# A dilated 7x7 convolution with softmax and gather: sorting of x shared anew, weights copied before the products, factors applied in other places

## The chip, the cores and the metric

The kernel runs on one core of a Trainium2 chip, in float32 throughout. The metric is the device time of one execution in microseconds (us). In the profile PE is TensorE (matmuls), PEld its loads of the stationary operand, DVE is VectorE, ACT ScalarE, POOL GpSimd, and SP the engine that issues most transfers. A "q" behind an engine's name is its sequencer, which issues transfers and waits.

## The reference, cut to what matters

```python
# x: (4, 256, 64, 64)
k = conv(x, w1, padding=6, rhs_dilation=2) + b1         # 128 channels, 7x7 taps
k = conv(k, w2) + b2                                    # 1x1: 49 channels
attn = softmax(k, axis=1)
xp = pad(x, 6)
shifts = stack([xp[:, :, 2*u:2*u+64, 2*v:2*v+64] for u in range(7) for v in range(7)], 1)
x = einsum('bkchw,bkhw->bchw', shifts, attn)            # gather
# second layer, a bottleneck with batch statistics
h = relu(bn(conv1x1(x, m1), g1, be1))
h = relu(bn(conv3x3(h, m2), g2, be2))
h = bn(conv1x1(h, m3), g3, be3)
out = relu(h + x)
```

No bias or activation stands between w1 and w2, so the kernel multiplies w1 by w2 first and convolves once, from 256 channels to 49 logits.

## The kernel before, in words

**The dilated convolution in passes.** Along the image's rows the seven taps are not multiplied one by one. Four numbers p (PAIRS = 0.4, 0.8, 1.25, 2.5) are points of a Toom-Cook scheme: for each pass the rows of x are summed with polynomial coefficients into two images, "even" and "odd" rows' sums mixed as x0 + p x1 and x0 - p x1; matmuls with weights evaluated at +p and -p follow, and the results are put together to four output rows. A fifth pass takes the points zero and infinity. Passes are numbered 0 to 4.

**Buffers.** One SBUF tile, `arena`, holds three regions: `slots`, the rows of x of 128 channels, sorted by parity so that a polynomial is a sum of shifted rows; `xi`, the two summed images of the pass at hand; and `ut`, the weights at all points. Columns are cut into four strips (32 columns of each column parity, eight to a strip). `visit` (L232) makes `xi` for some strips with `transform`, a series of multiply-adds on VectorE, all in the helper `stt` on L151. `apply_factor` (L226) works on `slots` in place: each row becomes the next row of its parity minus p^2 times the row, for a p whose pass is done, so that later passes have shorter sums. It is applied by parities (0 and 1) and strips. `column_convs(s)` (L251, matmuls on L262) adds one strip's products into eight PSUM banks: 200 matmuls for the four strips.

**Two halves of the channels.** The five passes run over the first 128 channels, and each pass's sums are put aside in DRAM (`put_aside`, L281, a copy on L286 and a transfer on L287, both on ScalarE). Then the five passes run over the other 128 channels. For these each strip's sums are put back into PSUM (`put_back`: a transfer on SP, L606, and a copy on ScalarE, L607), matmuls add to them, and `outputs` (copy L590 on ScalarE, L591 to L600 on VectorE) adds them into the four rows' logits.

**The opening.** x is loaded in twelve transfers (three pieces of rows times four images, `piece`, L344) and w1 in two times two (`load_w1`, L316). `sort_x` (L160) writes a piece into `slots` with four copies, recorded on L170: two parities k times two sub-rows a. Three run on ScalarE, and k=1, a=1 on GpSimd. `early` (L350) makes parts of pass 0's sums for the output rows that the pieces at hand allow. `product` (L319) forms the merged weights for one of seven columns of taps v: seven matmuls (L325) whose stationary operand is a slice of `w1raw` with a step of 49 elements, two evacuations on ScalarE (L336, L337), and two additions on VectorE (L341, L342). Seven products belong to the first half of the channels; after strips 0 and 1 of pass 0 the seven products of the second half follow on TensorE.

**What sets the order.** Within these stages the order of the instructions is that of the code: a manual schedule covers VectorE and TensorE in the first half, ScalarE and SP too in the opening (L365 on), and all four at the turns (L676 on). Each engine takes its own queue in order. GpSimd's order is the scheduler's. Small loads are issued on ScalarE's queue; those of `bn12` and `bn3` (L501 to L503) belong to tiles of the pool `keep`, made at the very start.

**Staging.** During passes 1 to 4 of the first half VectorE also prepares the second half: `fill_stage` sorts the other 128 channels into `stage`, `stage_parts` (L442) makes pass 0's sums for them, strip by strip into one buffer `stage_x`, and stores each as 1 MB in `ready_dram`; `stage_rows` (L450) stores the sorted rows in `fsort_dram`. The second half reads both.

**Turns.** After the softmax (`exponents` with the exponential on L527, `shares` with L534 to L540), `turn` (L555) transposes one half-strip's shares on TensorE (L566) and copies them into `amat`: for each of four j, part g=0 and part g=1, both on ScalarE (L573), except that with `shared` part g=1 is copied on VectorE (L571). The gather (L752) follows.

## Time and profile before

| | us |
|---|---|
| three runs | 800.84, 800.90, 802.21 |
| median | 800.9 |
| the profiled execution's own time | 799.53 |
| its span | 797.6 |
| TensorE busy | 729.1 |
| VectorE busy | 574.6 |
| ScalarE busy | 297.7 |
| GpSimd busy | 75.7 |

The span runs from the first to the last recorded instruction of the execution, and the execution's own time is 1.93 us longer. Times in the trace count from the start of the span. In round numbers the stages of the trace are: the opening to 55 us, pass 0 of the first half and the second half's products to 121.6, passes 1 to 4 to about 272, the second half to about 472, softmax and turns to about 499, gather and first 1x1 convolution to 657, and the rest of the bottleneck to 797.6. "A <- B" after a wait says that A stood idle until B had ended; a group's row in the profile's fifth part has its busy time, the mean of one instruction in ns, and the idle time before it.

### The profile page before, as it was taken

The numbers are of one execution on the slowest core, as the hardware profiler recorded it, in microseconds if no ns is written. First come the engines' busy times: TensorE is split into PE (matmuls) and PEld (weight loads), VectorE is DVE, ScalarE is ACT, GpSimd is POOL, SyncE is SP. The second block draws the span as 40 slices with busy tenths as digits, with TensorE's granted clock in tenths as the row PEclk, the third lists the DMA queues.
The fourth block names the chain that finished last, engine by engine and source line by source line (L and its number), as shares of the span: only waits on it lengthen the run. The fifth ranks groups of instructions, "written<-read, shape, count | busy, mean of one in ns | idle before, by whom it ended". The sixth has DMA issues, their size and how long they took to land.

```text
span 797.6 us, 10675 instructions
## 1 busy us (share of the span) xinstructions
PE 729.1 (91%) x4080; PEld 590.2 (74%) x4080; DVE 574.6 (72%) x682; ACT 297.7 (37%) x594; POOL 75.7 (9%) x143
## 2 busy tenths in 40 slices
PE   0949999999999999988999999999999979979996
PEld 0938977888888888867888888988887854438742
DVE  4489989999666999999999867233341337663697
ACT  4640155112551101110111158434442446345497
POOL 3210010001000020000002113222222200000000
PEclk9979999999999999998999999999999998998997
DMA  7941089913898886210210013666766669361298
GB/s 290 373 162 41 0 292 297 382 57 126 287 341 349 311 307 233 71 41 11 60 37 16 2 57 101 202 220 212 229 234 212 212 238 342 108 196 39 85 391 367
DMA packets 59236, 150.24 MB, mean 188 GB/s; under 512 B 7346, under 2 KB 35634, under 8 KB 55090
## 3 DMA queue, kind: packets, MB, share of 16 engines
q1 hardware_dynamic: 51216, 141.11, 49.7%
q10 hardware_dynamic: 7970, 8.45, 3.0%
q8 instruction: 32, 0.52, 0.3%
q14 instruction: 18, 0.15, 0.1%
HBM read 93.81 MB, written 55.74 MB: 188 GB/s over the span
## 4 chain that ended last, share of the span: by engine, by line
PE 72%; DVE 15%; ACT 5%; DMA 4%; issue 2%; POOL 0%; SPq 0%; ACTq 0%; DVEq 0%; POOLq 0%
PE acc L262 42%; PE acc L752 13%; DVE arena L151 9%; PE acc L785 4%; PE pconv L964 3%; PE pdirect L952 3%; DVE arena L1070 3%; PE acc L566 2%; PE moments L1030 2%; PE acc L325 2%; ACT outer L1075 1%; DMA outer<-in_xt_dram 1%; ACT arena L573 1%; DMA w1raw<-in_w_dram 1%; PE pturn L1026 1%
## 5 line engine op out<-in xcount | busy, mean ns | idle before, releaser
L262 PE MATMUL acc<-arena 128*128 128x343 f32 (+3 forms) x2000 | 380.2, 353 | 20.5 <-DVE arena L151 20.5
L262 PEld LDWEIGHTS acc<-arena 128*128 128x128 f32 x2000 | 321.6, 192 | 78.1 <-issue 15.7
L151 DVE SCALAR_TENSOR_TENSOR arena<-arena 128x1024 f32<-128x1024 f32 (+7 forms) x192 | 290.5, 1554 | 24.7 <-PE acc L262 14.2
L752 PEld LDWEIGHTS acc<-arena,outer 128*128 128x128 f32 x1024 | 116.0, 193 | 11.3 <-issue 10.1
L752 PE MATMUL acc<-arena,outer 128*128 128x128 f32 x1024 | 118.8, 277 | 3.1 <-issue 2.9
L793 DVE BATCH_NORM_STATS2 st<-acc 128x6 f32<-128x512 f32 x16 | 11.2, 699 | 68.2 <-PE acc L785 68.0
L286 ACT COPY sv<-acc 128x392 f32<-128x392 f32 x40 | 19.1, 484 | 99.2 <-PE acc L262 87.3
L170 ACT COPY stage<-raw 128x128 f32<-128x128 f32 x128 | 43.6, 415 | 23.9 <-DMA raw<-in_xp_dram 23.5
L325 PE MATMUL acc<-powers,w1raw 128*128 128x196 f32 (+1 forms) x196 | 45.3, 394 | 6.6 <-DMA w1raw<-in_w_dram 5.0
L325 PEld LDWEIGHTS acc<-powers,w1raw 128*128 128x128 f32 x196 | 44.5, 314 | 7.1 <-issue 7.0
L590 ACT COPY outer<-acc 128x784 f32<-128x784 f32 x8 | 6.5, 812 | 101.8 <-PE acc L262 101.8
L1013 PE MATMUL pconv<-arena,w3m 64*128 64x512 f32 (+1 forms) x144 | 43.0, 587 | 0.6 <-DVE arena L1070 0.6
L123 ACT COPY outer<-outer 64x2048 f32<-64x2048 f32 x15 | 28.4, 1895 | 38.4 <-DMA outer<-in_xt_dram 38.4
L151 DVE SCALAR_TENSOR_TENSOR outer<-outer 128x784 f32<-128x784 f32 (+2 forms) x47 | 36.8, 835 | 3.6 <-ACT outer L906 3.6
L1013 PEld LDWEIGHTS pconv<-arena,w3m 64*128 64x128 f32 x144 | 20.7, 185 | 21.9 <-DVE arena L1070 16.0
L1075 ACT ACTIVATE outer<-arena 128x512 f32<-128x512 f32 (+1 forms) x58 | 34.7, 695 | 1.3 <-DVE arena L849 1.1
L773 DVE COPY bks<-acc 128x256 f32<-128x256 f32 x32 | 11.3, 417 | 32.5 <-PE acc L752 32.5
L1070 DVE SCALAR_TENSOR_TENSOR arena<-pconv,arena 128x512 f32<-128x512 f32 (+1 forms) x58 | 34.3, 667 | 0.0
L124 POOL COPY outer<-outer 64x1792 f32<-64x1792 f32 x15 | 25.1, 1676 | 95.5 <-DMA outer<-in_xt_dram 80.1
L607 ACT COPY acc<-bks 128x392 f32<-128x392 f32 x40 | 18.5, 488 | 40.7 <-DVE outer L592 33.8
L573 ACT COPY arena<-acc 128x512 f32<-128x512 f32 x52 | 27.1, 708 | 14.8 <-PE acc L566 14.4
L964 PE MATMUL pconv<-outer,arena 128*128 128x512 f32 x72 | 31.1, 592 | 0.0
(143 smaller groups left out, 627.7 us busy)
## 6 DMA issues: line engine op xcount, KB each, us to landing
raw<-in_xp_dram SPq DMA_DIRECT2D x36, 608.0 KB, 5.3
outer<-in_xt_dram SPq DMA_DIRECT2D x17, 896.0 KB, 6.3
out_dram<-outer SPq DMA_DIRECT2D x14, 1024.0 KB, 4.5
arena<-y_dram SPq DMA_DIRECT2D x25, 512.0 KB, 7.9
fsort_dram<-stage SPq DMA_DIRECT2D x2, 4864.0 KB, 14.7
arena<-fsort_dram SPq DMA_DIRECT2D x8, 1216.0 KB, 10.0
y_dram<-outer SPq DMA_DIRECT2D x16, 512.0 KB, 5.4
aside_dram<-sv ACTq DMA_DIRECT2D x40, 196.0 KB, 5.7
```

What stands on the lines that cost most here:

```text
L123: nc.scalar.copy(t[:MID], x[MID:])
L151: nc.vector.scalar_tensor_tensor(out, in0, scalar, in1, ALU.mult, ALU.add)
L170: (last if last and k + a == 2 else nc.scalar.copy)(d[:, k, :, PLACE[b], 2 * a : 2 * a + 2, i : i + count], raw[:, lo : lo + 4 * count - 3 ...
L262: nc.tensor.matmul(acc[i][d][:, o : o + (hi - lo) * K], xi[:, i, CW * w : CW * w + CW, :].rearrange("p x t -> p (x t)"), u[i][:, lo * K : ...
L325: nc.tensor.matmul(pw[:, o : o + n], w1raw[:, :, u * K7 + v], powers[:, u, :n], start=(u == 0), stop=(u == K7 - 1), skip_group_check=True,)
L573: nc.scalar.copy(dst, src)
L752: nc.tensor.matmul(dst[:, :: NT - 1] if edge else pts[c][:, o : o + 128], x[:, i, half * P : (half + 1) * P], amat[:, b % 2, :, c, blocks, ...
L785: nc.tensor.matmul(pt[a * MID : (a + 1) * MID, :], w1m[:, n, :], ys[a, n][:, 512 * i : 512 * i + 512], start=(n == 0), stop=(n == NH - 1), ...
L964: nc.tensor.matmul(m[k], wu[:, k, j, :], vs[k][:, g, j : j + R, :], start=(j == 0), stop=(j == 1))
L1013: nc.tensor.matmul(pt[:, :n], w3m[part, half * P : (half + 1) * P], h2[part, slot, q, lo : lo + n], start=True, stop=True)
L1070: nc.vector.scalar_tensor_tensor(v, conv3(b, q, i, half, lo, n), sc3[:, half : half + 1], v, ALU.mult, ALU.add)
L1075: nc.scalar.activation(dst, v.rearrange("p (r w) -> p r w", w=R), AF.Relu, bias=sh3[:, half : half + 1])
```

## The change

- `bn12` and `bn3` become tiles of the pool `late`. Their ten loads are now issued after that of `w3m`, still on ScalarE's queue.
- `piece` is split into `load_piece` and `sort_piece`. In piece 1 of each image the copy k=0, a=0 runs on VectorE, in piece 2 on GpSimd, so that ScalarE has two of the four copies. Piece 2 is sorted by halves of the columns: strips 0 and 1 first, strips 2 and 3 after `early(1, strip(2, 2))`. The products of the first half and the calls of `early` are ordered anew among them.
- In a product of the second half, ScalarE first copies the seven taps (7 x 128 elements) out of `w1raw` into a buffer `w1v` of the pool of raw pieces, and the stationary operands are read from there, without a step.
- The factor of pass 1 is applied to strips 0 and 1, parity 0, ahead of pass 0's sums of strips 2 and 3; to parity 1 after the third product of the second half; and to strips 2 and 3 in pass 1, ahead of their `visit`.
- `stage_parts` stores each parity as soon as it is made, in two transfers of 0.5 MB.
- In turns (1, 1) and (2, 0) part g=1 of odd j is copied on VectorE: four copies.
- In the second half the factor of pass 2 is applied to strips 0 to 2 within pass 1, each after the next strip's `visit`; strip 3 keeps its place.

```diff
--- before.py
+++ after.py
@@ -101,8 +101,6 @@
 
 
     keep = pool(ctx, "keep", 1)
-    bn12 = keep.tile([P, 4], F32, name="bn12")
-    bn3 = keep.tile([P, 2, NH], F32, name="bn3")
     st1 = keep.tile([P, 2 * NT, 6], F32, name="st1")
 
 
@@ -157,7 +155,7 @@
 
     zero_rows(slots)
 
-    def sort_x(raw, b, r0, n, dst, w0, last=None):
+    def sort_x(raw, b, r0, n, dst, w0, last=None, first=None):
 
         d = dst.rearrange("p k (w b e) i -> p k w b e i", b=B, e=Q)
         nw = d.shape[2]
@@ -167,7 +165,7 @@
             i = (m + 3) // 2
             for a in range(2):
                 lo = 2 * m + a - r0
-                (last if last and k + a == 2 else nc.scalar.copy)(
+                (last if last and k + a == 2 else first if first and k + a == 0 else nc.scalar.copy)(
                     d[:, k, :, PLACE[b], 2 * a : 2 * a + 2, i : i + count],
                     raw[:, lo : lo + 4 * count - 3 : 4, PAD + 2 * w0 : PAD + 2 * w0 + 2 * nw].rearrange(
                         "p r (w c) -> p w c r", c=2
@@ -318,13 +316,19 @@
 
             def product(w1raw, half, v, pw):
 
+                wv = w1raw[:, :, v::K7].rearrange("p c u -> p u c")
+                if half:
+                    t = rawp.tile([P, 24, WP], F32, tag="raw", name="w1v").rearrange("p r w -> p (r w)")
+                    t = t[:, : K7 * P].rearrange("p (u c) -> p u c", c=P)
+                    nc.scalar.copy(t, wv)
+                    wv = t
                 for u in range(K7):
 
                     o = 0 if u == 0 else (2 + NP) * K if u % 2 else K
                     n = (1 + NP) * K if u in (0, K7 - 1) else NP * K
                     nc.tensor.matmul(
                         pw[:, o : o + n],
-                        w1raw[:, :, u * K7 + v],
+                        wv[:, u, :],
                         powers[:, u, :n],
                         start=(u == 0),
                         stop=(u == K7 - 1),
@@ -341,11 +345,16 @@
                 nc.vector.tensor_tensor(ut[:, half, 1 + NP : 1 + 2 * NP, c], ue, uo, ALU.subtract)
                 nc.vector.tensor_tensor(ue, ue, uo, ALU.add)
 
-            def piece(n, b):
+            def load_piece(n, b):
                 r0, k = PIECES[n]
                 raw = rawp.tile([P, 24, WP], F32, tag="raw", name="raw")
                 nc.sync.dma_start(out=raw[:, :k], in_=xp[b, :P, r0 : r0 + k, :])
-                sort_x(raw, b, r0, k, slots, 0, nc.gpsimd.tensor_copy)
+                return raw
+
+            def sort_piece(raw, n, b, cols=0, strips=NS):
+                r0, k = PIECES[n]
+                first = (None, nc.vector.tensor_copy, nc.gpsimd.tensor_copy)[n]
+                sort_x(raw, b, r0, k, slots[:, :, strip(cols, strips)], WS * cols, nc.gpsimd.tensor_copy, first)
 
             def early(n, cols=slice(None), parts=(even, odd, mix)):
 
@@ -364,47 +373,48 @@
             spare = [acc[i][s] for s in (NS - 1, 0) for i in range(2)]
             with tc.manual_schedule(engines={mybir.EngineType.Activation, mybir.EngineType.SP}):
                 for b in range(B):
-                    piece(0, b)
+                    sort_piece(load_piece(0, b), 0, b)
                 w1a = load_w1(0)
                 early(0)
                 nc.scalar.copy(b1row, b1sb.to_broadcast([P, P]))
                 nc.tensor.matmul(bank[7][:, :K], b1row, w2sb, start=True, stop=False)
                 nc.tensor.matmul(bank[7][:, :K], ones, b2sb, start=False, stop=True)
                 nc.scalar.copy(bias, bank[7][:, :K])
-                for b in range(2):
-                    piece(1, b)
-                    product(w1a, 0, b, bank[b])
-                for b in range(2, B):
-                    piece(1, b)
-                early(1, strip(0, 2), (even,))
-                for v in range(2, 5):
-                    if v > 2:
-                        piece(2, v - 3)
+                for b in range(B):
+                    if b == 3:
+                        product(w1a, 0, 0, bank[0])
+                    sort_piece(load_piece(1, b), 1, b)
+                for v, part in ((1, even), (2, odd)):
+                    early(1, strip(0, 2), (part,))
                     product(w1a, 0, v, bank[v])
-                early(1, strip(0, 2), (odd, mix))
-                piece(2, 2)
+                raws = []
+                for b in range(B):
+                    raws.append(load_piece(2, b))
+                    sort_piece(raws[b], 2, b, 0, 2)
+                early(1, strip(0, 2), (mix,))
+                product(w1a, 0, 3, bank[3])
+                product(w1a, 0, 4, bank[4])
+                early(2, strip(0), (even, odd))
                 product(w1a, 0, 5, bank[5])
-                piece(2, 3)
-                early(2, strip(0), (even, odd))
+                early(2, strip(0), (mix,))
                 product(w1a, 0, 6, bank[6])
-                early(2, strip(0), (mix,))
                 w1b = load_w1(1)
             early(2, strip(1))
             early(1, strip(2, 2))
+            for b in range(B):
+                sort_piece(raws[b], 2, b, 2, 2)
+            apply_factor(slots, squares[0], NR - 1, strip(0, 2), (0,))
             for s in range(2, NS):
                 early(2, strip(s))
             u = weights(0, 0)
             column_convs(0, u, True)
             column_convs(1, u, True)
             put_aside(0, 1)
-            product(w1b, 1, 0, spare[0])
-            apply_factor(slots, squares[0], NR - 1, strip(0, 2))
-            for v in range(1, 5):
+            for v in range(3):
                 product(w1b, 1, v, spare[v % 4])
-            apply_factor(slots, squares[0], NR - 1, strip(2, 2), (0,))
-            for v in range(5, K7):
+            apply_factor(slots, squares[0], NR - 1, strip(0, 2), (1,))
+            for v in range(3, K7):
                 product(w1b, 1, v, spare[v % 4])
-            apply_factor(slots, squares[0], NR - 1, strip(2, 2), (1,))
         for s in range(2, NS):
             column_convs(s, u, True)
             put_aside(0, s)
@@ -443,9 +453,9 @@
             for s in strips:
                 x = stgp.tile([P, 2, SW, NT], F32, tag="x", name="stage_x")
                 row = rows_of(stage, strip(s))
-                even(PAIRS[0], squares, row, x[:, 0])
-                odd(PAIRS[0], squares, row, x[:, 1])
-                nc.sync.dma_start(out=ready[:, 2 * h + s], in_=x)
+                for i, part in enumerate((even, odd)):
+                    part(PAIRS[0], squares, row, x[:, i])
+                    nc.sync.dma_start(out=ready[:, 2 * h + s, i], in_=x[:, i])
 
         def stage_rows(h):
             nc.sync.dma_start(out=fsort[:, h], in_=stage)
@@ -457,8 +467,8 @@
                 continue
             u = weights(n, 0)
             for h in range(2):
-                if factor is not None and factor != squares[0]:
-                    apply_factor(slots, factor, NR - 2, strip(2 * h, 2))
+                if factor is not None and (n, h) != (1, 0):
+                    apply_factor(slots, factor, NR - 1 if n == 1 else NR - 2, strip(2 * h, 2))
                 visit(slots, strip(2 * h, 2), p, left)
                 if (n, h) == (2, 1):
                     stage_parts(0, [0])
@@ -490,6 +500,8 @@
     w3m = late.tile([P, C], F32, name="w3m")
     pavg_sb = late.tile([P, P], F32, name="pavg_sb")
     pdiff_sb = late.tile([P, P], F32, name="pdiff_sb")
+    bn12 = late.tile([P, 4], F32, name="bn12")
+    bn3 = late.tile([P, 2, NH], F32, name="bn3")
     nc.scalar.dma_start(out=ident, in_=z)
     nc.scalar.dma_start(out=w1m, in_=m1t)
     nc.scalar.dma_start(out=pavg_sb, in_=pavg)
@@ -567,7 +579,7 @@
             for g in range(2):
                 dst = amat[:, g, 2 * (2 * s + h) + j % 2, j // 2].rearrange("p (n k) e -> p k n e", k=2)
                 src = pt[:, :, 64 * g : 64 * g + 64].rearrange("p (k w) n -> p k n w", k=2)
-                if shared and g:
+                if g and (shared or (j % 2 and (s, h) in ((1, 1), (2, 0)))):
                     nc.vector.tensor_copy(dst, src)
                 else:
                     nc.scalar.copy(dst, src)
@@ -630,10 +642,12 @@
             for t in pads:
                 nc.gpsimd.memset(t, 0.0)
         for s in range(NS):
-            if n == 2:
+            if n == 2 and s == NS - 1:
                 apply_factor(slots, factor, NR - 2, strip(s))
             if p is not None:
                 visit(slots, strip(s), p, left)
+            if n == 1 and s:
+                apply_factor(slots, passes[2][1], NR - 2, strip(s - 1))
             for d in ([s] if s == 0 else []) + ([s + 1] if s + 1 < NS else []):
                 put_back(n, d)
             column_convs(s, u, False)
```

## The prediction

> **What bounds the kernel now.** I read the page's busy shares first, then the waits, the chain of waits, and the busy time by windows of the stages that the change touches.
>
> ```profile
> PE 729.1 (91%) x4080; PEld 590.2 (74%) x4080; DVE 574.6 (72%) x682; ACT 297.7 (37%) x594; POOL 75.7 (9%) x143
> ```
>
> TensorE is busy for 91% of the span, so 68 us are all that a better order can win, and no edit here takes matmuls away. The waits (us in total, times, longest) say where VectorE holds TensorE up in the dilated conv:
>
> ```profile
> PE acc L262 <- DVE arena L151: 20.5, 3, 11.5
> ...
> DVE stage_x L151 <- DMA ready_dram<-stage_x: 6.2, 1, 6.2
> ```
>
> The trace puts the three at 43.4–54.9 (11.5), 118.6–121.6 (3.0) and 355.3–361.3 (6.0). The chain of waits (start, length) shows the two long stretches in which nothing but matmuls counts:
>
> ```profile
> 1.17 5.96 DMA b1sb<-in_b_dram
> 7.15 4.09 DMA raw<-in_xp_dram
> 11.26 9.69 DMA w1raw<-in_w_dram
> ...
> 121.63 224.88 PE acc L262 x1200
> ...
> 361.26 97.75 PE acc L262 x512
> ```
>
> What is won ahead of 121.63 reaches 346 only if VectorE keeps pace until then. The windows (PE, PEld, DVE, ACT, POOL busy, clock, DMA share, GB/s) tell how much room it has:
>
> ```profile
> 33.28:54.90 21.62, 10.90 (x50) 10.61 (x49) 16.81 (x25) 12.42 (x23) 4.65 (x4) 0.86 0.63 248
> 121.63:200.00 78.37, 78.37 (x415) 66.48 (x416) 77.75 (x36) 21.86 (x60) 2.56 (x4) 1.00 0.58 213
> 253.50:346.60 93.10, 93.10 (x496) 79.08 (x496) 89.87 (x68) 14.86 (x29) 3.99 (x1) 1.00 0.60 215
> ```
>
> In the opening VectorE idles 4.8 of 21.6 us; later it is as full as TensorE.
>
> **What the Trainium skill says.** "TensorE: Matmul & The Clock Gate", "LDWEIGHTS (loading the stationary operand)", has the load's time scale with the column count only. The trace disagrees for a strided source: 314 ns out of w1raw (elements 196 bytes apart, L325), 192 ns out of contiguous memory (L262); the measurement decides. "SBUF — State Buffer", "Door 1: The DMA port swizzle", says that an engine pays for each new 16-byte line. That agrees: the raw copies take 870 ns for 384 elements and spacings of 0.57 us for 256, some 1.75 ns per further element; the contiguous copy of L123 takes 1895 ns for 2048 (0.9). The same page, "Who interferes with whom", has VectorE with two SBUF inputs and GpSimd lock each other out; the trace agrees: GpSimd's 384-element copy takes 867 ns alone and 1420–1622 beside VectorE's additions, which then take 1477 and 1573 instead of about 1050.
>
> **The change part by part.** All times are the profiled execution's.
>
> ```profile
> L170 ACT COPY arena<-raw 128x384 f32<-128x384 f32 x24 | 19.1, 870 | 12.2 <-DVE arena L151 12.2
> ...
> L151 DVE SCALAR_TENSOR_TENSOR arena<-arena 128x4608 f32<-128x4608 f32 x4 | 19.7, 4951 | 0.0
> ```
>
> 1. *Tiny loads.* ACT's queue no longer begins with ten small loads, and in the built order raw loads 3 and 4 and the first w1 transfer wait for nothing; before, load 3 went out at 7.15, when b1 had landed. Up to the end of w1a 5.70 MB move at 396 GB/s (window 13–33): 14.4 us and some 4 for issue and first landing, 18.4 instead of 20.95, **−2.4**. The pieces of x follow on SP's queue, whose order of loads doesn't change.
> 2. *Sorting.* ACT copies 2 of 4 parts of a piece instead of 3, 1.6 us instead of 2.4; VectorE takes one of a piece 1 (estimate 0.45 each, from its 0.41 for 245–256 elements), GpSimd a second of a piece 2. A piece lands each 2.3 us, so sorting ends with the last landing. The first even addition on rows of piece 1 starts at about 28.4 instead of 33.28 (**−4.9**: 2.4 from the landings, 2.5 from ACT, which stood behind products). Of the 4.8 us idle some 3 stay, while piece 2's halves arrive: **−6.5** where strips 0 and 1 are done.
> 3. *Factor moved forward.* One 4.95 us apply (parity 0 of strips 0, 1) and about 1 of lock with GpSimd's copies come ahead of strips 2 and 3: the early sums end at 81.0 (before 81.46). This eats the gain on VectorE, but moves it off what follows.
> 4. *To pass 1.* Before, 28 us lie between: four applies and 14 additions of weights to 110.0, then the visit to 123.9. After: additions 14 × 0.38 = 5.3, one apply 4.95 and about 1 waiting for products, so the visit starts at 92.3 and ends at 106.2. TensorE's products, contiguous now (a matmul pair 0.33–0.36 instead of 0.44, seven per product), which ended at 99.7, end at an estimated 89.4; strips 2, 3 take 18.9 (99.69–118.60): pass 1 starts at 108.3 instead of 121.63, **−13.3**.
>    *The new copies w1v* stand on ACT ahead of each product: 896 elements, 0.93 us by the price (224 + elements)/1.2 ("VectorE: DVE Perf Modes", "The TRN2 errata table"), 1.7 us by the trace's strided 1.75 ns. I take 1.7. A product needs 2.4–3.1 us of TensorE and the copies have two spare buffers, so up to 2 us each they are hidden; without cover they cost 7 × the excess.
> 5. *Given back at pass 1, second pair of strips.* The two applies of strips 2, 3 are now here: 106.2 + 9.9 + visit 13.9 = 130.0; TensorE is ready at 108.3 + 18.75 (half of a pass of 37.5) = 127.05 and waits 3.0. It went on at 121.63 + 18.75 = 140.4 before: **−10.4**. From there TensorE is solid, and VectorE's 7.7 and 6.5 us waits on it (214.8, 230.6) show that it has room again; the shift stays until 346.
> 6. *Second half.* The stage in two transfers: the wait of 6.2 us at 253.5 is for a 1 MB store issued at 247.4; with halves, the first is out earlier. VectorE gains about 1.3, but it must stay ahead of TensorE only to 346. Pass 2's applies of strips 0–2 move into pass 1: the same work. Two things lose. The ten tiny loads now follow the late loads on ACT's queue:
>
> ```profile
> 288.12 0.34 ACTq L493 DMA_DIRECT2D ident<-in_z_dram  x1
> ...
> 290.06 1.20 ACTq L499 DMA_DIRECT2D w3m<-in_m3t_dram  x2
> 291.30 0.81 ACT L590 COPY outer<-acc 128x784 f32<-128x784 f32 x1 [19.14 <-PE acc L262]
> 292.14 0.49 ACT L607 COPY acc<-bks 128x392 f32<-128x392 f32 x1
> ```
>
>    Ten issues at about 0.5 hold L590 and the copies put back (L607) by 5; they start earlier by 9, so TensorE waits 0.9 more. And the stop before pass 2 becomes 7.4 + 0.8 in place of 6.0 + 1.5: +0.7. Together **+1.6**: −8.8.
> 7. *Turns.* The chain around the turns, and what stands on VectorE:
>
> ```profile
> 482.27 0.97 DVE L534 TENSOR_REDUCE sm<-outer 128x16 f32<-128x784 f32 x1 [0.40 <-ACT outer L527]
> 482.74 10.03 ACT L573 COPY arena<-acc 128x512 f32<-128x512 f32 x20
> ...
> 484.00 4.03 PE L566 MATMUL acc<-ident,outer 128*128 128x128 f32 x32 [1.36 <-ACT arena L573]
> ...
> 491.33 3.19 DVE L571 COPY arena<-acc 128x512 f32<-128x512 f32 x5 [2.90 <-ACT arena L573]
> ```
>
>    Two copies of turn (1,1) and two of (2,0) go to VectorE, ahead of shares(3) in the order written out by hand. The last waits for transposes that end at 488.0, and takes 0.7. shares(3), which ran 482.3–487.4, now runs 488.7–493.7, and behind it stand the copies of turn (2,1). The transposes of (3,0), which need their banks, start at about 495 instead of 492.07: **+2.9**. That ACT has four copies (2.0) less doesn't help, since the queue that ends last is VectorE's.
>
> Sum: −10.4 + 1.6 + 2.9 = **−5.9**. After the turns nothing is changed. Against the execution's own time (span 797.6, 1.9 around it, 799.5) that is 793.6. The runs' median is 1.4 above it: **795.0**.
>
> **Rivals.** *A, the ledger above:* 795.0.
> *B, the turns cost nothing:* VectorE's copies find their transposes ready because the shift leaves it ahead, or the gain on ACT counts. For it: TensorE's wait at 484.00 is for ACT. Against it: shares(3) has no second place to go. 795.0 − 2.9 = 792.1.
> *C, the tiny loads bite late:* a [128,1] load has packets of 4 bytes, and the one in the opening took 5.96 us. If each issue holds ACT's queue longer than 0.5 (beside row loads that fill the DMA), L590 and L607 come late and TensorE stops between strips. Beyond about 5 us the excess counts: 9 us in all would give back 4.9 (9 + the 0.9 above, less the 5 that are free), so 799.9. Against it: the late loads before issue at 0.34–0.6 each.
> *D, slower, by w1v:* seven copies of 896 elements with 196-byte steps stand on ACT one behind the other, with the two evacuations of each product (0.57) between. The products come just ahead of strips 2, 3 on TensorE. From 3.0 us a copy the whole gain is gone: 7 × (3.0 − 1.7) = 9.1, less the 3.0 that TensorE waits for VectorE anyway, is the 5.9 forecast. At 3.5 us each, 12.6 − 3.0 − 5.9: slower by 3.7, 804.6. For it: no row shows a copy with such a step, and 3.5 ns per element is twice the nearest row. Against it: that row already has a new line for each element.
>
> **How the numbers follow.** A 0.62, B 0.14, C 0.15, D 0.09. Time shown is A's. What a measurement can tell from no change is about 0.2%, 799.3–802.5. A and B are faster, a tenth of A and C's lower part too; C's rest is within 0.2%, D slower: 0.81, 0.10, 0.09. Range: from B less 1 (the opening's unknown costs: sorting, lock, 1 us either way), 790.5, to C, 800.0. It leaves out D and the ends of B and C.
>
> **What would show it.** Right: the first w1 landing at 18–19; pass 1's first matmul at 108–109; a stop of 3–4 us about 19 us later; no TensorE wait from there to 280; a shift of 9 at the last pass, of 6 at the gather. w1v's copies should read 0.9–2 us. Wrong: copies over 3 us; TensorE waits on L607 between strips of the second half; (3,0) starting without a wait for VectorE; or a stop at strips 2, 3 of pass 0 because products end later than 90.

## The result and the profile after

| | before | after |
|---|---|---|
| median of 20 runs, us | 800.87 | 799.24 |
| ratio of the times | | 0.9978 (95%: 0.9965 to 0.9992) |
| the profiled execution's own time | 799.53 | 799.82 |
| its span | 797.6 | 798.0 |

The change gains 1.6 us where 5.9 were forecast. (The two profiled executions lie 1.3 below and 0.6 above their medians, so their spans show even less.) Lines have moved: L260 is the conv's matmul (before L262), L149 `stt` (L151), L578/L583/L585 the turns (L566/L571/L573), L602 and L619 the copies of `outputs` and `put_back` (L590, L607).

The busy shares after, and then TensorE's and the other engines' waits (us in total, times, longest):

```profile
PE 727.9 (91%) x4080; PEld 588.4 (74%) x4080; DVE 582.2 (73%) x690; ACT 303.4 (38%) x597; POOL 89.8 (11%) x155
```

```profile
DVE stage_x L149 <- DMA ready_dram<-stage_x: 5.5, 1, 5.5
...
PE acc L260 <- DVE arena L149: 10.0, 3, 7.5
...
PE acc L260 <- ACT acc L619: 3.6, 3, 1.9
...
PE acc L578 <- DVE arena L583: 3.4, 1, 3.4
```

TensorE's waits for VectorE in the conv were 20.5, now 10.0 and, under another name (for the weights' additions, L346), 7.3 in the opening. But three waits are new: 3.6 for the copies put back, 3.4 at the turns, and part of the 10.0 stands at another place. TensorE's timeline shows where (start, length, what, idle before it):

```profile
89.49 37.63 PE L260 MATMUL acc<-arena 128*128 128x147 f32 x200
128.13 0.90 PE L260 MATMUL acc<-arena 128*128 128x147 f32 x6 [1.02 <-DVE arena L149]
130.46 9.75 PE L260 MATMUL acc<-arena 128*128 128x147 f32 x37 [1.43 <-DVE arena L149]
```

```profile
292.03 3.90 PE L260 MATMUL acc<-arena 128*128 128x196 f32 x16 [1.90 <-ACT acc L619]
297.11 1.30 PE L260 MATMUL acc<-arena 128*128 128x49 f32 x8 [1.18 <-ACT acc L619]
298.96 34.43 PE L260 MATMUL acc<-arena 128*128 128x49 f32 x188 [0.55 <-ACT acc L619]
340.91 115.21 PE L260 MATMUL acc<-arena 128*128 128x147 f32 x600 [7.52 <-DVE arena L149]
```

To follow the lead, I number the 2000 matmuls of the conv in each trace and subtract the start times of the same number (after minus before, us from each span's start):

| matmul, its time before | lead after |
|---|---|
| first, 55.65 | −7.0 |
| pass 1's first, 121.63 | −13.4 |
| 149.80, behind pass 1's second pair of strips | −8.9 |
| 271.47, the second half's first | −8.9 |
| 309.23, the second half's pass 0 nearly done | −4.0 |
| 318.19, past it | −4.5 |
| 392.62, behind both halves' last stops | −2.9 |
| 470.85, the conv's last | −2.9 |
| 499.12, the gather's first | +1.7 |
| 797.59, end | +0.4 |

The opening won 13.4, and four places gave it back: 4.5 behind pass 1's first pair, 4.4 at the start of the second half, 1.6 at its stop for VectorE, 4.6 at the turns. Behind the gather's start 1.3 come back, and not by the change: at 611.86 the granted clock of the execution before stands at half for 3.41 us, where that of the changed kernel stays full.

### The profile page after: what moved, and what is told of

Read it like the earlier page. It is cut to its first block, busy times and chain, and to the rows that moved or that the text cites. A ratio compares the mean times of both kernels' runs of the same rounds, so it can differ in the third digit from the quotient of the medians.

```text
span 798.0 us, 10702 instructions
## 1 busy us (share of the span) xinstructions
PE 727.9 (91%) x4080; PEld 588.4 (74%) x4080; DVE 582.2 (73%) x690; ACT 303.4 (38%) x597; POOL 89.8 (11%) x155
## 4 chain that ended last, share of the span: by engine, by line
PE 55%; DVE 25%; DMA 9%; ACT 5%; issue 3%; SPq 0%; POOL 0%; ACTq 0%; DVEq 0%; POOLq 0%
PE acc L260 29%; DVE arena L149 13%; PE acc L766 11%; DVE arena L1084 4%; PE acc L799 4%; PE pconv L978 3%; PE pdirect L966 3%; DMA outer<-in_xt_dram 2%; DMA raw<-in_xp_dram 2%; PE moments L1044 2%; DMA fsort_dram<-stage 2%; PE acc L578 2%; ACT arena L585 2%; DVE stage_x L149 2%; ACT arena L168 1%
## 5 line engine op out<-in xcount | busy, mean ns | idle before, releaser
L260 PE MATMUL acc<-arena 128*128 128x343 f32 (+4 forms) x2000 | 383.3, 354 | 20.9 <-DVE arena L149 10.0
L260 PEld LDWEIGHTS acc<-arena 128*128 128x128 f32 x2000 | 323.3, 193 | 79.8 <-DVE arena L149 10.5
L149 DVE SCALAR_TENSOR_TENSOR arena<-arena 128x1024 f32<-128x1024 f32 (+6 forms) x192 | 293.2, 1568 | 22.2 <-PE acc L260 15.9
L602 ACT COPY outer<-acc 128x784 f32<-128x784 f32 x8 | 6.5, 812 | 105.3 <-PE acc L260 77.9
L121 ACT COPY outer<-outer 64x2048 f32<-64x2048 f32 x15 | 28.4, 1896 | 38.1 <-DMA outer<-in_xt_dram 38.1
L149 DVE SCALAR_TENSOR_TENSOR outer<-outer 128x784 f32<-128x784 f32 (+2 forms) x47 | 36.8, 835 | 3.6 <-ACT outer L920 3.6
L619 ACT COPY acc<-bks 128x392 f32<-128x392 f32 x40 | 18.5, 488 | 41.6 <-DVE outer L604 29.5
L585 ACT COPY arena<-acc 128x512 f32<-128x512 f32 x48 | 25.5, 657 | 21.0 <-PE acc L578 20.9
L168 POOL COPY arena<-raw 128x192 f32<-128x192 f32 (+2 forms) x24 | 25.3, 1084 | 40.4 <-DVE arena L149 24.4
L799 PE MATMUL acc<-outer,w1m 128*64 128x512 f32 x64 | 29.6, 600 | 0.0
## 6 DMA issues: line engine op xcount, KB each, us to landing
arena<-fsort_dram SPq DMA_DIRECT2D x8, 1216.0 KB, 10.1
```

The costliest lines, as they stand in the source:

```text
L121: nc.scalar.copy(t[:MID], x[MID:])
L149: nc.vector.scalar_tensor_tensor(out, in0, scalar, in1, ALU.mult, ALU.add)
L168: (last if last and k + a == 2 else first if first and k + a == 0 else nc.scalar.copy)(d[:, k, :, PLACE[b], 2 * a : 2 * a + 2, i : i + count],
L260: nc.tensor.matmul(acc[i][d][:, o : o + (hi - lo) * K], xi[:, i, CW * w : CW * w + CW, :].rearrange("p x t -> p (x t)"), u[i][:, lo * K : ...
L585: nc.scalar.copy(dst, src)
L799: nc.tensor.matmul(pt[a * MID : (a + 1) * MID, :], w1m[:, n, :], ys[a, n][:, 512 * i : 512 * i + 512], start=(n == 0), stop=(n == NH - 1), ...
```

## The experiments

Each kernel is the changed one with the edit shown. Ratios are to the kernel before, run beside it on the same chip. The changed kernel's 0.9978 is the mark; it comes from a series of its own, so a difference of two ratios carries both intervals. "Lead" is TensorE's lead over the kernel before, as in the table above.

**The ten loads back at the beginning.**

```diff
     keep = pool(ctx, "keep", 1)
+    bn12 = keep.tile([P, 4], F32, name="bn12")
+    bn3 = keep.tile([P, 2, NH], F32, name="bn3")
...
-    bn12 = late.tile([P, 4], F32, name="bn12")
-    bn3 = late.tile([P, 2, NH], F32, name="bn3")
```

> The changed kernel with the ten loads of bn12 and bn3 back at the beginning of ScalarE's queue. If these loads, late in that queue, are what stops the second half's first pass (TensorE lost 4.4 us of its lead between 281 and 305), the waits of its matmuls for the copies put back (3.6 us) are gone or under 1, at most 1 us of the lead is lost there, and the opening loses at most the 2.4 us that I gave to the earlier landing of w1a: 1 to 3 us faster than the changed kernel, some 796.5. If those waits come from the row loads that fill the DMA, they stay, and the kernel is 0 to 2.4 us slower than the changed one.

Measured: 0.9963 (0.9949 to 0.9977). The waits for L619 are gone and no lead is lost from 149.8 to 318.2 (−7.3, −7.3). The opening has 3.2 less lead than the changed kernel (−3.8 at the first matmul), more than the 2.4 allowed for. Both parts of the move are thus seen in the trace: it wins some 3 us at the start and loses 4.4 at the middle. In time the two kernels are not apart.

**The ten loads behind the second half's w1.** The tiles are as in the last kernel, the loads are issued at the end of the opening's block:

```diff
                 w1b = load_w1(1)
+                for half in (slice(0, MID), slice(MID, P)):
+                    for i, a in enumerate((g1, be1, g2, be2)):
+                        nc.scalar.dma_start(out=bn12[half, i : i + 1], in_=a[:, None])
+                nc.scalar.dma_start(out=bn3[:, 0, :], in_=g3.rearrange("(n p) -> p n", p=P))
+                nc.scalar.dma_start(out=bn3[:, 1, :], in_=be3.rearrange("(n p) -> p n", p=P))
```

> The changed kernel with the ten loads neither at the very beginning nor behind w3m, but on ScalarE's queue behind the issue of the second half's w1, at about 50 us, where ScalarE has nothing urgent. If the late loads cost their place alone, the opening keeps its lead (7.0 at the first matmul of the convolution, 13.4 at pass 1) and the second half's first pass loses none; what is won there meets VectorE in pass 1 of the second half, as with the loads at the beginning, so that the convolution ends 5 to 6.5 us ahead of the kernel before and the whole is 1.5 to 3.5 us faster than the changed one. If any ten loads hold ScalarE by their landings, some of this is lost at 50 to 60 us: pass 0 starts later than 49.5.

Measured: 0.9929 (0.9908 to 0.9950), so 0.5% faster than the changed kernel. The opening keeps all of its lead (−7.2, −13.5), none is lost up to 318.2 (−10.6), and the conv ends 8.6 ahead. That is more than the 5 to 6.5 expected: behind 318.2 the stops for VectorE take 2.0 of the lead, as they do with the loads at the beginning (2.1, from a smaller lead), and don't take back what was won ahead of them.

**The ten loads on GpSimd's queue, late as in the change.**

```diff
-            nc.scalar.dma_start(out=bn12[half, i : i + 1], in_=a[:, None])
-    nc.scalar.dma_start(out=bn3[:, 0, :], in_=g3.rearrange("(n p) -> p n", p=P))
-    nc.scalar.dma_start(out=bn3[:, 1, :], in_=be3.rearrange("(n p) -> p n", p=P))
+            nc.gpsimd.dma_start(out=bn12[half, i : i + 1], in_=a[:, None])
+    nc.gpsimd.dma_start(out=bn3[:, 0, :], in_=g3.rearrange("(n p) -> p n", p=P))
+    nc.gpsimd.dma_start(out=bn3[:, 1, :], in_=be3.rearrange("(n p) -> p n", p=P))
```

> The changed kernel with the ten late loads issued by GpSimd instead of ScalarE, at the same place of the program; nothing of them is left in ScalarE's queue. If what stops the second half's first pass is ScalarE held back by their issue and landings (and SP's row loads, which wait for landings of the same loads), the lead lost at 281 to 305 falls from 4.4 to under 1.5. If it is their 4-byte packets in the DMA engines, it stays at 3 to 4.4.

Measured: 0.9900 (0.9871 to 0.9928), and the lead from 149.8 to 318.2 falls by 0.2, from 10.1 to 9.9. So the packets themselves cost next to nothing there; issuing them on ScalarE's queue does. The timeline of that queue in the changed kernel (a "q" line is an issue):

```profile
278.82 0.34 ACTq L505 DMA_DIRECT2D ident<-in_z_dram  x1
279.19 0.46 ACTq L506 DMA_DIRECT2D w1m<-in_m1t_dram  x1
...
281.93 0.62 ACTq L513 DMA_DIRECT2D bn<-in_be_dram  x1
284.21 0.47 ACTq L513 DMA_DIRECT2D bn<-in_g_dram  x1
...
287.96 0.91 ACTq L513 DMA_DIRECT2D bn<-in_be_dram  x1
289.69 0.38 ACTq L514 DMA_DIRECT2D bn<-in_g_dram  x1
290.12 0.48 ACTq L515 DMA_DIRECT2D bn<-in_be_dram  x1
290.64 0.81 ACT L602 COPY outer<-acc 128x784 f32<-128x784 f32 x1 [27.36 <-DMA bn<-in_be_dram]
291.48 0.49 ACT L619 COPY acc<-bks 128x392 f32<-128x392 f32 x1
```

and with the loads on GpSimd's:

```profile
277.85 0.34 ACTq L505 DMA_DIRECT2D ident<-in_z_dram  x1
...
279.84 1.19 ACTq L511 DMA_DIRECT2D w3m<-in_m3t_dram  x2
281.07 0.81 ACT L602 COPY outer<-acc 128x784 f32<-128x784 f32 x1 [18.99 <-PE acc L260]
281.91 0.49 ACT L619 COPY acc<-bks 128x392 f32<-128x392 f32 x1
```

L602 follows the first issue by 11.8 us in one, by 3.2 in the other: ten loads hold ScalarE by 8.6, not 5. Two gaps in the queue make most of the difference, 1.7 us at 282.6 and 0.8 at 288.9. In the changed kernel's chain the first ends with a landing:

```profile
278.82 5.37 DMA ident<-in_z_dram
284.19 0.02 issue
284.21 0.47 ACTq L513
284.68 0.04 issue
284.72 5.15 DMA bn<-in_be_dram
289.87 0.02 SPq L436
```

In the trace the transfers of ScalarE's and SP's queues share eight completion counters (semaphores that tell of a landing), and an issue waits until the transfer that had its counter last has landed. The issue at 284.21 follows the landing of ident at 284.19, that at 289.69 a landing at 289.67. So a load of a few bytes can cost more than its issue: of the 8.6 us the ten issues are some 6, and two waits for landings 2.5. SP is held as well: the last lines show its load of the ready parts (L436) released by a bn load. SP's transfers for `put_back`, behind it, went out at 290.77; two of TensorE's three waits for L619 come behind them. GpSimd's ten loads have eight counters of their own, so this run moves the queue and the counters together and doesn't tell them apart.

**The turns as before the change.**

```diff
-                if g and (shared or (j % 2 and (s, h) in ((1, 1), (2, 0)))):
+                if g and shared:
```

> The changed kernel with the four copies of turns (1,1) and (2,0) back on ScalarE. If the copies hold up shares(3) on VectorE and so the transposes of (3,0), TensorE's wait of 3.4 us for VectorE there goes, the clock fall of 3.4 us at half speed right behind it goes too, and the gather starts 4.6 us earlier; 2.5 to 4.6 us faster than the changed kernel. If the gather is held by its loads of x anyway, the time stays within 1 us.

Measured: 0.9930 (0.9908 to 0.9953), 0.5% faster than the changed kernel. The lead is 5.7 at the conv's end and 5.7 at the gather, and 5.35 of it reach the end: the gather is not held by its loads. The timeline of the changed kernel shows the four copies, then shares(3), then the copies of turn (2,1), then the transposes of (3,0):

```profile
485.99 0.69 DVE L583 COPY arena<-acc 128x512 f32<-128x512 f32 x1 [0.78 <-ACT arena L585]
486.59 0.96 DVE L546 TENSOR_REDUCE sm<-outer 128x16 f32<-128x784 f32 x1
...
490.26 1.18 DVE L552 TENSOR_TENSOR outer<-outer,sm 128x196 f32<-128x196 f32 x4
491.36 3.24 DVE L583 COPY arena<-acc 128x512 f32<-128x512 f32 x5
...
492.10 8.87 PE L578 MATMUL acc<-ident,outer 128*128 128x128 f32 x64 [3.44 <-DVE arena L583]
```

The 64 transposes take 8.87 us; in the kernel before they took 7.2. Behind the wait the granted clock is half (the column before DMA share, from the windows of the changed kernel):

```profile
130.46:134.60 4.14, 4.14 (x14) 3.45 (x15) 4.14 (x1) 1.20 (x4) 0.00 (x0) 0.59 1.07 449
493.00:496.50 3.50, 3.50 (x19) 3.50 (x18) 2.22 (x4) 1.17 (x2) 1.00 (x5) 0.51 0.81 277
```

The first window lies behind the wait at 128 to 130, the second behind that at the turns. With the turns undone, the transposes run at full clock:

```profile
130.46:134.60 4.14, 4.07 (x20) 3.38 (x21) 4.14 (x2) 0.80 (x2) 0.00 (x0) 1.00 1.18 493
484.00:490.00 6.00, 5.88 (x52) 5.40 (x51) 4.03 (x7) 4.80 (x10) 2.31 (x11) 1.00 0.70 230
```

This kernel is the changed one up to the turns, yet its clock at 130 to 134 is full and its lead at 149.8 is 10.5 instead of 8.9. The half clock behind that wait comes in some executions only.

**Work for TensorE during pass 1's wait.**

```diff
+                if (n, h) == (1, 1):
+                    for r in range(12):
+                        nc.tensor.matmul(
+                            acc[0][1][:, WS * K :],
+                            xi[:, 0, CW * (WS + r % WS) : CW * (WS + r % WS) + CW, :].rearrange("p x t -> p (x t)"),
+                            u[0][:, : 512 - WS * K],
+                            start=False, stop=False, skip_group_check=True,
+                        )
                 for s in range(2 * h, 2 * h + 2):
```

> The changed kernel with twelve extra matmuls of 120 columns ahead of strip 2 of pass 1, into columns of a bank that nothing reads: TensorE has work for some 2.5 us of its wait for VectorE. If the half clock behind this wait (3.4 us, 1.6 lost, in one execution of the changed kernel, not in that with the turns undone) comes of the idle time, the clock stays full there and the lead at 150 us is 10.5 or a little less instead of 8.9. If it comes of something else, it falls as before. The end moves by at most 1.6 us.

Measured: 0.9970 (0.9956 to 0.9984); lead 10.8 at 149.8 and the clock full. By itself this decides nothing, since kernels with the same wait and without this work kept the full clock there as well: that with the turns undone (lead 10.5), and those with the loads behind w1b (10.6) and on GpSimd's queue (10.1).

The traces side by side show what does decide it. In each of the 14, the falls of the clock start on a grid of 3.413 us, to within 0.001 us, and the place of the grid differs from execution to execution. TensorE's busy time in a window of that grid goes with the clock in the next:

| kernel, wait | window, us | TensorE busy in it, us | clock in the next |
|---|---|---|---|
| changed, pass 1 | 127.78–131.19 | 1.63 (48%) | half |
| turns undone, pass 1 | 124.91–128.32, 128.32–131.73 | 2.36 (69%), 1.98 (58%) | full, full |
| changed, turns | 489.59–493.00 | 0.90 (26%) | half |
| pass 2's factor undone (below), turns | 481.99–485.40, 485.40–488.81 | 1.75 (51%), 1.63 (48%) | full, full |

Between 40 and 760 us the 14 traces have 67 windows at full clock in which TensorE was busy for less than 42%, and half clock follows all of them; it follows none of the 2707 above 55%, and 10 of the 29 between. The same wait thus costs a fall or not by how the grid happens to cut it. The extra matmuls filled the wait, so that no window there was under 55%.

**Pass 1's strips 2 and 3 apart.**

```diff
-                if factor is not None and (n, h) != (1, 0):
-                    apply_factor(slots, factor, NR - 1 if n == 1 else NR - 2, strip(2 * h, 2))
-                visit(slots, strip(2 * h, 2), p, left)
+                for s, k in ((2, 1), (3, 1)) if (n, h) == (1, 1) else ((2 * h, 2),):
+                    if factor is not None and (n, h) != (1, 0):
+                        apply_factor(slots, factor, NR - 1 if n == 1 else NR - 2, strip(s, k))
+                    visit(slots, strip(s, k), p, left)
```

> The changed kernel, in pass 1 of the first half with factor and visit of strips 2 and 3 one strip after the other instead of both together: the same sums in twice as many instructions of half the size. If the lost 4.4 us of lead at 127 to 141 are TensorE's wait for VectorE (2.5) and the half clock behind it (1.7), strip 2 is ready before TensorE gets there, both go, and TensorE's lead over the kernel before stays at 13 to 280. What comes of it in the end is 1 to 4.4 us, less what the store of the sorted rows (15 us, ahead of the second half) gives back. If VectorE's load sets the pace from there, the lead shrinks to the same 9 within the next passes.

Measured: 0.9969 (0.9957 to 0.9981), not apart from the changed kernel. The wait at 128 is gone (lead 13.9 at 149.8), and two come in its place within the next pass, of 1.7 and 0.9 us at 147 and 168: the lead settles at 10.8. VectorE's load sets it there: the wait at 128 was mostly work that VectorE owed anyway, and cost little of its own.

**Products without w1v.**

```diff
-                if half:
+                if False:
```

> The changed kernel with the second half's products reading w1raw in place, without the seven copies. If the copies shorten the weight loads (314 to 192 ns), the 49 matmuls of these products take 4 to 5 us longer without them and pass 1 starts 4 to 5 later; 2.5 of that meets the wait of pass 1's second half, whose clock fall then goes as well: 0 to 1 us slower than the changed kernel. If the copies cost more on ScalarE than they bring, the products end earlier than 89.5 and the kernel is faster.

Measured: 1.0000 (0.9985 to 1.0015), so the copies bring 0.2%, at the edge of what these runs can tell. Without them the lead at pass 1 is 10.8 instead of 13.4, and 7.0 instead of 8.9 at 149.8; the clock fall there, which was expected to go, is in this execution too. In the changed kernel the copies take 1.8 us each, and the loads from them 189 ns instead of 314:

```profile
L329 PEld LDWEIGHTS acc<-powers,w1v x98: 186/189/192, 69.3 to 89.1; 128*128 128x128 f32 x98
...
L323 ACT COPY w1v<-w1raw x7: 1803/1821/1867, 64.3 to 78.3; 128x896 f32<-128x896 f32 x7
```

**Each stage in one store.**

```diff
-                for i, part in enumerate((even, odd)):
-                    part(PAIRS[0], squares, row, x[:, i])
-                    nc.sync.dma_start(out=ready[:, 2 * h + s, i], in_=x[:, i])
+                even(PAIRS[0], squares, row, x[:, 0])
+                odd(PAIRS[0], squares, row, x[:, 1])
+                nc.sync.dma_start(out=ready[:, 2 * h + s], in_=x)
```

> The changed kernel with each stage stored in one transfer of 1 MB again. I gave the two transfers 1.3 us on VectorE. If they matter, VectorE's wait for the store (5.5 us at the change, 6.2 before) is 1 to 2 us longer, and the second half starts up to 1.3 us later; at most 1.3 us slower. If the wait is for room in the DMA and not for the last byte, the same within 1 us.

Measured: 0.9978 (0.9955 to 1.0001), the same. VectorE's wait for the store is 6.1 with one transfer and 5.5 with two: 0.6, where the prediction gave 1.3.

**Pass 2's factor back in pass 2.**

```diff
-            if n == 2 and s == NS - 1:
+            if n == 2:
                 apply_factor(slots, factor, NR - 2, strip(s))
...
-            if n == 1 and s:
-                apply_factor(slots, passes[2][1], NR - 2, strip(s - 1))
```

> The changed kernel with pass 2's factor of strips 0 to 2 back in the second half's pass 2. If moving it forward made the stop of 7.8 us ahead of strip 3 of pass 1 (VectorE has three applies of 2.4 to do first), this stop goes, and one of some 6 us or less at pass 2's second strip comes back, as before: the convolution ends 0 to 2 us earlier than in the changed kernel. If VectorE's whole load up to there sets the time, the stop only changes its place and the time is the same within 1 us.

Measured: 0.9906 (0.9890 to 0.9922), 0.7% faster than the changed kernel, an effect as large as that of the loads on GpSimd's queue within the noise. TensorE's stop of 7.5 us is replaced by a shorter one, at pass 2's second strip:

```profile
317.60 31.34 PE L260 MATMUL acc<-arena 128*128 128x343 f32 x166
352.70 3.67 PE L260 MATMUL acc<-arena 128*128 128x147 f32 x11 [3.76 <-DVE arena L149]
```

Over this stretch (318.2 to 392.6) the lead grows from 6.2 to 7.8; in the changed kernel it falls from 4.5 to 2.9. VectorE shows why. In the changed kernel, from 331.55 to the end of the stop, and in this one, up to its own:

```profile
328.01 3.63 DVE L149 SCALAR_TENSOR_TENSOR outer<-outer 128x784 f32<-128x784 f32 x4
331.55 13.84 DVE L149 SCALAR_TENSOR_TENSOR arena<-arena 128x1024 f32<-128x1024 f32 x10
```

```profile
329.51 10.43 DVE L149 SCALAR_TENSOR_TENSOR arena<-arena 128x1024 f32<-128x1024 f32 x7
340.38 0.97 DVE L603 TENSOR_TENSOR outer<-acc,outer 128x784 f32<-128x784 f32 x1 [0.43 <-PE acc L260]
```

Among these, each apply is two instructions of 2.42 us, one for each parity. (In the second half VectorE's order is the scheduler's; the edit sets from where on it may place them.) In the first kernel four of these instructions, 9.7 us of work for pass 2, run between 319 and 340, among and ahead of the visit of pass 1's last strip, for which TensorE waits from 333 to 341. In the second, one runs at 320 and two at 334 to 340, behind that visit, and TensorE works on to 349; there its wait is for pass 2's second strip. In this execution too the transposes of (3,0) start 2.9 late by the turns' copies (lead 7.8, then 4.9), without a clock fall.

**Edits together.** First the ten loads behind w1b, the turns undone and the strips apart:

> The changed kernel with three edits together: the ten loads behind the second half's w1, the turns' copies as before the change, and factor and visit of pass 1's strips 2 and 3 one after the other. If the three losses are separate, the gather starts 7 to 9 us ahead of the kernel before; 7 to 9 us faster than that, some 5 to 7 faster than the changed kernel. If VectorE's load takes back in the second half what the first wins, it is no faster than the kernel with the turns alone undone, 5.6 us ahead of the kernel before.

Measured: 0.9879 (0.9857 to 0.9901); the gather starts 9.4 ahead. Then also pass 2's factor back in pass 2:

> The three edits of the kernel before this one (ten loads behind the second half's w1, turns as before the change, strips 2 and 3 of pass 1 apart), and pass 2's factor back in pass 2. If moving the factor into pass 1 makes the stop of VectorE longer by itself, the two stops of 2.4 and 4.7 us at 317 and 330 become one of about 4 or less and the gather starts 10.5 to 12.5 us ahead of the kernel before instead of 9.4. If the three edits have already taken what it won (TensorE is kept by VectorE's whole load), it stays at 9 to 9.5.

Measured: 0.9830 (0.9799 to 0.9861); the gather starts 11.65 ahead, and the two stops at 317 and 330 are one of 4.5. And that without the strips apart:

> The same without the edit of pass 1's strips 2 and 3. If VectorE's load sets when pass 2 of the second half goes on, the gather starts as early as with it, within 1 us: TensorE's wait of 3 us at 127 only takes the place of a longer stop in the second half. If TensorE's lead is kept, it starts 2 to 4 us later.

Measured: 0.9817 (0.9782 to 0.9852); the gather starts 10.3 ahead, 1.35 less than with the strips; the times are not apart. These two beat the kernel before by 1.7 and 1.8%, and the changed one by 1.5 and 1.6%.

## Why the prediction was wrong

The direction was right, the size was not: 5.9 forecast, 1.6 measured.

**Steps 1 to 4 held.** The first product starts at 18.3 (18.4 forecast), the first even sum of piece 1 at 28.43 (28.4), the conv 7.0 earlier (6.5), products end at 89.5 (89.4), pass 1 starts at 108.2 (108.3), and a copy w1v takes 1.8 us (1.7). Rival D is out. Three slips stand in the working, none of which moves its total: 18.4 instead of 20.95 is 2.55 less, not 2.4; in D, 9.1 less 3.0 is 6.1, not 5.9; and 870 ns for 384 elements beside 570 for 256 make 2.3 ns per further element, not 1.75. From 384 elements to the 896 of a copy w1v it measured 1.86.

**Step 5 was right on the wait and left out what follows it.** TensorE went on at 130.46 (130.0). But in the profiled execution the clock then stood at half for 3.4 us, which took the lead from some 10.5 to 8.9. This is no fixed price: of the nine kernels that have the wait and no extra matmuls in it, only the changed one and the one without w1v show the fall, each behind a window in which TensorE was busy for 48 or 49%.

**Step 6, +1.6 forecast, +6.0 measured, is the step that failed,** in both its terms.
- *"Ten issues at about 0.5 hold L590 and the copies put back (L607) by 5; they start earlier by 9, so TensorE waits 0.9 more."* They held them by 8.6 and not by 5: the ten issues took some 6, two waits for landings 2.5, and they held SP's queue too. TensorE lost 4.4 instead of 0.9. This is rival C, to which I gave 0.15. Its sum gives 4.5 for a hold of 8.6 (8.6 + 0.9 − 5); its reason, longer issues, is the smaller part. The experiments with the loads earlier and on GpSimd's queue show it: 0.0 and 0.2 lost. That C's 799.9 lies near the measured 799.2 is in part luck, since C has neither the loss at pass 2's factor nor the two clock falls in its sum. The profile of before had it to be read: its chain begins with a raw load on SP that starts only when b1 has landed. I used that for step 1 and not for step 6.
- *"Pass 2's applies of strips 0–2 move into pass 1: the same work ... +0.7."* It is the same work, ahead of what TensorE needs next, on an engine that is behind. The stop itself was forecast well (7.4, measured 7.5, against 6.0 before); the saving of 0.7 set against it (0.8 in place of 1.5) did not come. This stretch took 1.6 of the lead; with the applies back it gives 1.6. Undone alone, it brings 0.7%.

**Step 7 was right on the wait, +2.9, and again not on the clock.** The execution with a full clock shows 2.9 to the tenth (that with pass 2's factor undone); the changed kernel's has the half clock behind the wait, 4.6 in all. Eight of the nine kernels with these copies have it. The Trainium skill, "TensorE: Matmul & The Clock Gate", section "What's actually happening", has a window of about 3.4 us that runs freely, and half clock after an idle one. The traces agree on the window: falls of 3.4, 6.8 and 10.2 us on a grid of 3.413. They differ on the idle: half clock came behind every window in which TensorE was busy for less than 42%, and behind some of those at full clock up to 55%; the measurement decides. A wait of 3.4 us leaves such a window unless the grid cuts it near its middle, as in the one execution without a fall (51 and 48% busy). The waits of 1.0 and 1.4 us close together leave one only where the grid happens to fall so. Which way it goes in a single execution is chance.

**The sum.** −5.9 becomes −5.9 + 1.6 (clock at pass 1) + 4.4 (step 6) + 1.7 (clock at the turns) = +1.8 at the gather, where +1.7 was measured; 1.3 come back behind it by the clock fall of the execution before, and the medians stand 1.9 better than the two profiled executions. What each part is worth by the timed runs: loads behind w1b −0.5% (on GpSimd's queue −0.8%, not apart), pass 2's factor −0.7%, turns −0.5%; all three together −1.6%, which is about their sum. The gain of the opening was there. It was spent at pass 1's second pair of strips, which was forecast but for the clock, and by the late loads, pass 2's factor and the turns. Of these three only the move of the loads had won any of it, some 3 us, and behind w1b the loads keep that without the price.

## What to carry to other kernels

A small load moved to a "free" place takes a turn in its engine's queue and in whatever limits transfers in flight: price it by its issue and by the landing that this may have to wait for, and look which copies stand behind it and whether another queue waits for it too. On an engine that another is waiting for, work for later goes behind what is needed next, even where the total is the same. And a wait of TensorE of some 3 us is to be counted with a second price, the half clock behind it (1.7 us here), as a chance: the same wait, cut in another place by the clock's windows, goes free.

## What the runs showed of the hardware beyond that

- Ten loads of a kilobyte or less, issued one behind another with six larger ones, kept ScalarE from 278.8 to 290.6: 11.8 us, of which 3.2 are the six larger. On GpSimd's queue the same ten took 0.2 us of TensorE's lead.
- A granted clock of one half lasted 3.4 us or a multiple of it in every trace here, at 1.7 us per 3.4 where TensorE was busy throughout. Kernels with the same instructions up to a point differ by one such fall (the changed kernel and that with the turns undone, 8.9 and 10.5 at 149.8). Three traces have one at 82.6 to 83.2, among the second half's products, which cost about 2 there.
